# Window attention's values turned by DMA: sixteen transfers in one go, in long pieces, and an earlier wait on TensorE

## The chip, the cores and the metric

The kernel runs on one core of a Trainium2 chip, in 32-bit floating point. The metric is the device time of one execution in microseconds (us); lower is better.

## What is computed

The input x has 16 images of 56 x 56 positions with 384 channels. Two layers follow each other, each added to its input:

```python
x = x + window_attention(group_norm(x))   # 12 heads of 32, windows of 7 x 7, shifted by 3
x = x + depthwise_conv3x3(group_norm(x))  # 3 x 3 weights of +1, 0 or -1 for each channel
```

The attention, for each window of 49 positions and each head:

```python
q, k, v = split(x @ w_qkv.T)                  # 384 -> 3 x 384
score = q @ k.T / sqrt(32) + relative_bias    # 49 x 49, with masks in edge windows
out = softmax(score) @ v                      # 49 x 32
out = out @ w_out.T + b_out
```

The change is about v on its way to the product with the softmax.

## The kernel before, in words

**Tiling.** An image is cut into 8 strips of 7 rows (392 positions, 8 windows). There are 128 strips, numbered s. Each strip has two units of four windows; u = 2s is the first half, u = 2s + 1 the second. A unit takes about 15 us, an image about 242.

**One strip's attention.** TensorE forms queries and keys (`query_key`, L471, tile `pq`) and values (`value`, L483, tile `pv`) with channels on the partitions; ScalarE copies them to `qk` and `vt`. For each unit, `scores` (L515) multiplies keys with queries into `score_banks`, VectorE adds the bias (L546), ScalarE takes the exponential (L564, tile `e`), `add_up` (L592) sums it over the keys with a product by ones (L599), `attend` (L608) multiplies the exponentials with the values (L619, tile `po`), ScalarE copies the result (L629). In between, ScalarE and VectorE invert the sums (L637 to L640), and VectorE multiplies the result with them (L647). After both halves `project` (L649, tile `py`) applies w_out, and VectorE adds the input (L666).

**The values by key.** The product in `attend` needs the values with the keys on the partitions. `turn` (L496) has VectorE transpose 32 x 32 blocks of `vt` into `vq`, where a partition still belongs to a group of 32 channels' heads. `by_key` (L503) then moves blocks of 32 partitions by DMA from `vq` to the tile `v` (two buffers): 16 transfers a strip, each of 32 partitions and 48 KB, in two parts of eight. In `v`, the 32 channels of a head are put at their place among 384, so a transfer's piece is 32 numbers, 128 bytes.

**The order of the work** is written out by hand. `heavy` (L939) lists for each unit six steps; `all_units` (L973) runs a step's list, and between the steps what is planned for that time from the other layers (convolution, loads, stores). In the first unit of strip s, the values of strip s + 1 are formed in steps 0, 1 and 2, turned in steps 1, 2 and 3, and `by_key` comes in step 3 (part 0) and step 5 (part 1). Right after step 0 of each unit come `add_up` and `attend`. So TensorE's order in a first half is: three products of `pv`, the sums, the products with the values, the rest of `pv`, the scores of the next unit, `pq`; in a second half `pq`, sums, products, `pq`, then `py` and scores.

**Queues.** The transfers of `by_key` are issued by SyncE. In the same queue, in the order of the program, lie the convolution's loads of a band (`band`, L705) and its stores (`store`, L800), eight for a chunk. The loads of the next image's strips and the stores of the middle result lie on GpSimd's queue (L421, L682). SyncE takes its instructions one after the other: one that waits holds up those behind it.

**Waits.** The scheduler puts the waits for other engines and for DMAs on the instruction that first needs them. The sixteen transfers of a strip count on eight semaphores, two transfers each. An instruction that has more than one wait gets instructions of its own in front of it, shown as EVENT_SEMAPHORE, which TensorE's sequencer executes. In the kernel before, the values' waits lie on the first eight products of `attend` in a strip's first half.

**The convolution** of image b - 1 goes on beside the attention of image b, mostly on VectorE (`tap`, L786), in chunks of 2.6 units.

Of the kernel before, what the change touches and what calls it, by code (L numbers as in the profile page):

```python
# [9 lines left out]
F32 = mybir.dt.float32  # L10
# [24 lines left out]
def kernel(  # L35
# [12 lines left out]
    nc = tc.nc  # L48
    P = 128
    B, H, W, C = x.shape  # L50
    NH = rel_table.shape[1]
    D = C // NH
    NC = C // P
    HPC = P // D
    T = WIN * WIN
    NS = H // WIN
    NW = W // WIN
    ST = WIN * W
    UW = 4
    UPS = NW // UW  # L60
# [22 lines left out]
    vpool = ctx.enter_context(tc.tile_pool(name="v", bufs=2))  # L83
# [9 lines left out]
    def bank(name):  # L93
        return ps.tile([P, 512], F32, tag="mm", name=name)
# [21 lines left out]
    vq = const.tile([P, 4, NW // 2, NC, D], F32, tag="vq", name="vq")  # L116
# [121 lines left out]
    stats, coefs, parts = {}, {}, {}  # L238
# [124 lines left out]
    xs = {}  # L363
# [93 lines left out]
    vs, ots, pts, ys = {}, {}, {}, {}  # L457
    raw, sums = {}, {}
# [37 lines left out]
    def turn(s, m):  # L496

        nc.vector.transpose(  # L498
            vq[:, :, :, m].rearrange("p h n d -> p n h d"),
            vt[:, m].rearrange("p (n w) (j b) -> p n (w j) b", w=2, b=D),  # L500
        )

    def by_key(s, part):  # L503

        if part == 0:
            vs[s] = vpool.tile([P, NW // 2, C], F32, tag="v", name=f"v_{s}")
        v = vs[s]
        for half in range(2 * part, 2 * part + 2):
            for i in range(HPC):
                nc.sync.dma_start(  # L510
                    v[half * D : (half + 1) * D].rearrange("k n (m c) -> k (n m) c", m=NC)[:, :, i * D : (i + 1) * D],
                    vq[i * D : (i + 1) * D, half].rearrange("k n m d -> k (n m) d"),
                )

    def scores(u, fast):  # L515


        s, n = divmod(u, UPS)
        pp = score_banks
        rows = T if fast else HT  # L520
        for j in range(NC):
            for r in range(2):
                for k in range(2 * HPC):
                    i, w = k % HPC, (k + k // HPC) % 2
                    part = slice(i * D, (i + 1) * D)
                    q0 = (n * UW + 2 * r + w) * T
                    row, col = (w, r) if fast else (r, w)
                    k0 = (2 * j + col) * T
                    nc.tensor.matmul(  # L529
                        pp[row * HT : row * HT + rows, i, k0 : k0 + T],  # L530
                        qk[part, NC * fast + j, q0 : q0 + rows],
                        qk[part, NC * (not fast) + j, q0 : q0 + T],
                        start=True,
                        stop=True,
                    )
        raw[u] = pp
# [50 lines left out]
    def by_head(u):  # L587

        flat = es.rearrange("k h w q -> k (h w q)")[:, : NH * 2 * T]
        return flat.rearrange("k (h r q) -> k h r q", h=NH, r=2)  # L590

    def add_up(u):  # L592

        flat = es.rearrange("k h w q -> k (h w q)")[:, : NH * 2 * T]
        su = raw[u][:, 0:2, : NC * 2 * T]
        for i in range(HPC):
            for w in range(2):
                keys = slice(w * HT, w * HT + T)
                nc.tensor.matmul(  # L599
                    su[i * D : (i + 1) * D, w],  # L600
                    ones[keys, :D],
                    flat[keys, i * NC * 2 * T : (i + 1) * NC * 2 * T],
                    start=True,
                    stop=True,
                )
        sums[u] = su

    def attend(u, fast):  # L608
        s, n = divmod(u, UPS)
        if n == 0:  # L610
            ots[s] = two.tile([P, NC, ST], F32, tag="ot", name=f"ot_{s}")
        po = [bank(f"po_{u}_{w}") for w in range(2)]
        for j in range(NC):
            for r in range(2):
                for i in range(HPC):
                    for w in range(2):
                        h = HPC * j + i
                        keys = slice(w * HT, w * HT + T)
                        nc.tensor.matmul(  # L619
                            po[w][i * D : (i + 1) * D, (2 * j + r) * T : (2 * j + r + 1) * T],  # L620
                            vs[s][keys, n * 2 + r, h * D : (h + 1) * D],
                            by_head(u)[keys, i * NC + j, r] if fast else pts[u, j][keys, 2 * i + r, :],
                            start=True,
                            stop=True,
                        )
        ot = ots[s][:, :, n * UW * T : (n + 1) * UW * T]
        by_window = ot.rearrange("p j (r w q) -> p j r w q", r=2, w=2)
        for w in range(2):
            nc.scalar.copy(  # L629
                by_window[:, :, :, w, :], po[w][:, : NC * 2 * T].rearrange("p (j r q) -> p j r q", j=NC, r=2)  # L630
            )
# [55 lines left out]
    mids, bands, outs, centers = {}, {}, {}, {}  # L687
# [45 lines left out]
    count, padded = [0], {}  # L733
# [205 lines left out]
    def heavy(u):  # L939

        s, half = divmod(u, UPS)
        todo = [[] for _ in range(2 * NC)]
        more = s + 1 < B * NS
        for m in range(NC):
            if half == 0 and more:
                todo[m].append((value, (s + 1, m)))
                todo[m + 1].append((turn, (s + 1, m)))
                todo[NC + m].append((query_key, (s + 1, m)))
            if half and more:
                todo[m].append((query_key, (s + 1, NC + m)))  # L950
            if half:
                todo[NC + m].append((project, (s, m)))
        if more and not half:
            for part in range(2):
                todo[NC + 2 * part].append((by_key, (s + 1, part)))
        if half and s + 2 < B * NS:
            todo[NC + 1].append((normalize, (s + 2,)))
        return todo
# [14 lines left out]
    def all_units(fast):  # L973
        for m in range(2 * NC):
            query_key(0, m)
        scores(0, fast)
        softmax(0, fast)
        for m in range(NC):
            value(0, m)
        normalize(1)  # L980
        exponential(0, fast)
        for m in range(NC):
            turn(0, m)
        for part in range(2):
            by_key(0, part)
        plan(nc.sync)
        for u in range(B * NU):
            todo = heavy(u)
            light = [(w, f, a) for w, f, a in sorted(side.pop(u, []), key=lambda i: i[0])]
            more = u + 1 < B * NU  # L990

            then = NC if u % UPS else NC - 1
            for i in range(len(todo)):
                run(todo[i])
                if i == 0:
                    if fast:
                        add_up(u)
                    else:
                        for j in range(NC):
                            transpose(u, j)  # L1000
                    if fast:
                        invert(u)
                    attend(u, fast)
                    if fast:
                        divide(u)
                if i == then and more:
                    scores(u + 1, fast)
                    softmax(u + 1, fast)
                if i == then + 1 and more:
                    exponential(u + 1, fast)  # L1010
                while light and light[0][0] - u <= (i + 1) / len(todo):
                    _, g, a = light.pop(0)
                    g(*a)
            for _, g, a in light:
                g(*a)
        for _, g, a in sorted((i for u in side for i in side[u]), key=lambda i: i[0]):
            g(*a)
        side.clear()
# [47 lines left out]
    with tc.If(redo != 0):  # L1066
        with tc.manual_schedule():
            staged.clear()
            for kept in (xs, stats, coefs, parts, vs, ots, pts, ys, raw, sums, mids, bands, outs, centers, padded):
                kept.clear()  # L1070
            clear_again()
            load_bias(nc.gpsimd, 0, T, False)
            add_bias(False)
            for s in range(2):
                fetch(s)
            for s in range(NS):
                for c in range(NC):
                    load(s, c)
                if s + 2 < NS:
                    fetch(s + 2)  # L1080
            norm_gather((0, 0), nc.sync)
            norm_scale((0, 0), nc.sync, nc.vector)
            normalize(0)
            all_units(False)
# [44 lines left out]
```

## Time and profile before

| | |
|---|---|
| time, median of 3 runs | 4079.17 us (4078.88 to 4080.06) |
| profiled execution | 4081.16 us, span 4079.4 us |
| TensorE clock granted | 0.991 of full speed, mean |
| busy: PE, PEld, DVE, ACT, POOL | 98%, 60%, 86%, 55%, 46% |
| DMA packets | 1523990, of these 1458970 under 512 bytes |
| transfers v<-vq | 2048 of 48.0 KB |
| waiting instructions of L619 | 949 |

PE is TensorE's matmul, PEld its weight loads, DVE is VectorE, ACT ScalarE, POOL GpSimd, SP SyncE; a q behind the name means the engine's sequencer. A matmul in 32 bits shows as two records of PE and two of PEld: the 48 products of a unit are 96 records. The starts of records are measured; their ends on TensorE are modelled. A row of the timeline gives start, length, engine, line, operation, tiles and the number of records merged, and in brackets the idle time before it with what ended it. The timeline's length of a row runs to the end of its last record.

### The profile page before, as it was taken

What the parts mean: (1) busy time and instruction counts of PE and PEld (TensorE: products, weight loads), DVE (VectorE), ACT (ScalarE), POOL (GpSimd) and SP (SyncE); (2) the same over time, 40 slices, a digit from 0 to 9 for tenths busy, and PEclk for the clock granted to TensorE, in tenths of its full rate; (3) what the DMA queues carried; (4) which work ended last, traced back from release to release, by engine and by line L of the source; (5) the groups of instructions that cost most, each with busy time, mean ns of one, the idle gap of its engine ahead of it and who ended that gap; (6) DMA issues with size and microseconds to landing.
All of it is one profiled execution on the core that took longest, in us unless ns stands there. A gap on an engine that the chain in (4) does not pass through costs nothing.

```text
span 4079.4 us, 144987 instructions
## 1 busy us (share of the span) xinstructions
PE 3981.1 (98%) x63161; PEld 2447.1 (60%) x63161; DVE 3495.8 (86%) x3712; ACT 2231.7 (55%) x4654; POOL 1870.2 (46%) x3165
## 2 busy tenths in 40 slices
PE   5999999999999999999999999999999999999997
PEld 3666666656656666566666666666566566666656
DVE  4555989889898998989889898998989889898897
ACT  2555646555565655656555565655656556565552
POOL 5444535545453554545445452554545455452100
PEclk8999999999999999999999999999999999999998
DMA  4434556655665665556665665655556565664544
GB/s 95 78 62 90 112 102 127 107 109 107 114 114 111 117 111 108 111 99 128 108 116 104 113 117 105 117 117 101 115 101 123 105 124 104 108 123 79 108 102 110
DMA packets 1523990, 438.93 MB, mean 108 GB/s; under 512 B 1458970, under 2 KB 1473979, under 8 KB 1523346
## 3 DMA queue, kind: packets, MB, share of 16 engines
q1 hardware_dynamic: 1432680, 267.66, 38.9%
q0 software_dynamic: 87648, 159.12, 16.4%
q8 instruction: 500, 8.19, 0.9%
q10 hardware_dynamic: 3018, 2.78, 0.3%
q14 instruction: 144, 1.18, 0.1%
HBM read 169.63 MB, written 158.46 MB: 80 GB/s over the span
## 4 chain that ended last, share of the span: by engine, by line
PE 46%; issue 16%; POOL 12%; DVE 12%; DMA 7%; SPq 4%; ACT 2%; DVEq 0%; ACTq 0%; POOLq 0%
PE pq L474 19%; PE pv L487 10%; PE py L658 8%; POOL xl L421 8%; DVE o L786 5%; PE score_banks L529 3%; PE po L619 3%; SPq L510 3%; DMA xl<-in_x_dram 2%; PE score_banks L599 2%; DMA mvd<-mv 2%; DVE e L546 1%; POOL dev L270 1%; DMA gt<-mvd 1%; DVE xt L438 1%
## 5 line engine op out<-in xcount | busy, mean ns | idle before, releaser
L474 PE MATMUL pq<-xn,wq_t 128*128 128x392 f32 x4608 | 1586.7, 497 | 0.1
L421 POOL DMA_DIRECT2D xl<-in_x_dram x1980 | 1329.3, 722 | 153.8 <-DVE xt L438 94.2
L786 DVE SCALAR_TENSOR_TENSOR o<-hp,dw_t,o 128x1568 f32<-128x1568 f32 x752 | 1378.4, 1833 | 5.7 <-DVE o L786 0.5
L474 PEld LDWEIGHTS pq<-xn,wq_t 128*128 128x128 f32 x4608 | 846.1, 188 | 596.1 <-issue 1.4
L487 PE MATMUL pv<-xn,wq_t 128*128 128x392 f32 x2304 | 815.9, 497 | 9.8 <-DVE y L666 8.6
L658 PE MATMUL py<-ot,wo_t 128*128 128x392 f32 x2304 | 818.2, 500 | 4.8 <-DVE ot L647 3.8
L481 ACT COPY qk<-pq 128x392 f32<-128x392 f32 x768 | 368.4, 482 | 609.6 <-PE pq L474 609.3
L678 POOL COPY y<-y 128x63 f32<-128x63 f32 x128 | 59.4, 464 | 1280.5 <-DVE y L666 1280.5
L487 PEld LDWEIGHTS pv<-xn,wq_t 128*128 128x128 f32 x2304 | 424.2, 189 | 309.9 <-DVE y L666 10.4
L658 PEld LDWEIGHTS py<-ot,wo_t 128*128 128x128 f32 x2304 | 425.8, 190 | 306.5 <-DVE ot L647 20.1
L564 ACT ACTIVATE e<-e 128x1176 f32<-128x1176 f32 x256 | 303.3, 1185 | 462.5 <-DVE e L546 461.4
L639 DVE SCALAR_TENSOR_TENSOR ln<-score_banks,inv 128x588 f32<-128x588 f32 x256 | 195.9, 765 | 349.2 <-ACT inv L638 349.2
L494 ACT COPY vt<-pv 128x392 f32<-128x392 f32 x384 | 188.8, 492 | 393.0 <-PE pv L487 392.1
L619 PEld LDWEIGHTS po<-e,v 49*32 49x32 f32 x24576 | 352.2, 105 | 60.4 <-issue 14.3
L619 PE MATMUL po<-e,v 49*32 49x49 f32 x24576 | 347.1, 212 | 13.4 <-DMA v<-vq 11.9
L546 DVE SCALAR_TENSOR_TENSOR e<-score_banks,bias 128x1176 f32<-128x1176 f32 x256 | 347.2, 1356 | 10.7 <-PE score_banks L529 10.7
L529 PEld LDWEIGHTS score_banks<-qk 32*49 32x49 f32 x24576 | 265.7, 118 | 145.4 <-issue 108.9
L450 ACT COPY x<-xt 128x196 f32<-128x196 f32 x720 | 225.5, 368 | 176.0 <-DVE xt L438 175.6
L529 PE MATMUL score_banks<-qk 32*49 32x49 f32 x24576 | 298.2, 218 | 2.6 <-DVE ln L639 2.2
L498 DVE STREAM_TRANSPOSE vq<-vt 128x512 f32<-128x512 f32 x384 | 265.6, 693 | 9.9 <-ACT vt L494 6.4
L463 ACT ACTIVATE xn<-x,coef 128x392 f32<-128x392 f32 x384 | 247.1, 711 | 13.3 <-DMA coef<-cod 13.3
L666 DVE TENSOR_TENSOR y<-py,x 128x392 f32<-128x392 f32 x384 | 213.3, 555 | 43.1 <-PE py L658 39.2
(174 smaller groups left out, 3279.3 us busy)
## 6 DMA issues: line engine op xcount, KB each, us to landing
v<-vq SPq DMA_DIRECT2D x2048, 48.0 KB
xb<-mid SPq DMA_DIRECT2D x90, 855.5 KB
out_dram<-o SPq DMA_DIRECT2D x736, 98.0 KB
mid<-y POOLq DMA_DIRECT2D x112, 619.5 KB
xl<-in_x_dram POOLq DMA_DIRECT2D x1260, 52.5 KB
mid<-y POOLq DMA_DIRECT2D x15, 354.0 KB
xl<-in_x_dram POOLq DMA_DIRECT2D x180, 28.0 KB
mid<-y POOLq DMA_DIRECT2D x15, 265.5 KB
```

The costliest lines, as they stand in the source:

```text
L421: nc.gpsimd.dma_start(xz[i * D + lo : i * D + hi, c, k : k + n, :], flat[token : token + n * (hi - lo)].rearrange("(k t) c -> t k c", k=n) ...
L463: nc.scalar.activation(xn[:, c, :, :T], xs[s][:, c, :].rearrange("p (w t) -> p w t", t=T), AF.Identity, bias=coef[:, c, 1:2], scale=coef[: ...
L474: nc.tensor.matmul(pq[:, :ST].rearrange("p (w t) -> p w t", t=T), wq_t[:, c, m * P : (m + 1) * P], xn[:, c, :, :T], start=(c == 0), stop=( ...
L481: nc.scalar.copy(qk[:, m, :ST], pq[:, :ST])
L487: nc.tensor.matmul(pv[:, :ST].rearrange("p (w t) -> p w t", t=T), wq_t[:, c, 2 * C + m * P : 2 * C + (m + 1) * P], xn[:, c, :, :T], start= ...
L498: nc.vector.transpose(vq[:, :, :, m].rearrange("p h n d -> p n h d"), vt[:, m].rearrange("p (n w) (j b) -> p n (w j) b", w=2, b=D),)
L529: nc.tensor.matmul(pp[row * HT : row * HT + rows, i, k0 : k0 + T], qk[part, NC * fast + j, q0 : q0 + rows], qk[part, NC * (not fast) + j, ...
L546: nc.vector.scalar_tensor_tensor(e, pp[:, :, : NC * 2 * T].rearrange("q i (n k) -> q i n k", k=T), QSCALE, bias[:, int(s % NS == NS - 1)]. ...
L564: nc.scalar.activation(flat, flat, AF.Exp, accum_out=reach[:, 0, u : u + 1])
L619: nc.tensor.matmul(po[w][i * D : (i + 1) * D, (2 * j + r) * T : (2 * j + r + 1) * T], vs[s][keys, n * 2 + r, h * D : (h + 1) * D], by_head ...
L658: nc.tensor.matmul(py[:, :ST], wo_t[:, c, m * P : (m + 1) * P], ots[s][:, c, :], start=(c == 0), stop=(c == NC - 1),)
L786: nc.vector.scalar_tensor_tensor(acc, by_half(hp[:, dy : dy + BR, dx : dx + W]), dw_t[:, c, t : t + 1], acc, ALU.mult, ALU.add)
```

## The change

All sixteen transfers of a strip are issued in one call of `by_key`, in step 3 of the unit. The tile `v` is laid out anew, as key, group of 32 partitions, window pair, third of the heads, channel of the head, so that each partition's 384 numbers of a transfer lie together: the piece is 1536 bytes. `attend` reads the same 32 numbers for each head at their new place. And the first product of `add_up` in a strip's first half is made to wait for all sixteen transfers (but for the very first strip), by a dependency that is added by hand; the products of `attend` behind it then need no wait of their own for them.

```diff
-    def by_key(s, part):
-
-        if part == 0:
-            vs[s] = vpool.tile([P, NW // 2, C], F32, tag="v", name=f"v_{s}")
-        v = vs[s]
-        for half in range(2 * part, 2 * part + 2):
+    carried = {}
+
+    def by_key(s):
+
+        vs[s] = vpool.tile([P, HPC, NW // 2, NC, D], F32, tag="v", name=f"v_{s}")
+        carried[s] = []
+        for half in range(4):
             for i in range(HPC):
-                nc.sync.dma_start(
-                    v[half * D : (half + 1) * D].rearrange("k n (m c) -> k (n m) c", m=NC)[:, :, i * D : (i + 1) * D],
-                    vq[i * D : (i + 1) * D, half].rearrange("k n m d -> k (n m) d"),
+                move = nc.sync.dma_start(
+                    vs[s][half * D : (half + 1) * D, i].rearrange("k n m d -> k (n m d)"),
+                    vq[i * D : (i + 1) * D, half].rearrange("k n m d -> k (n m d)"),
                 )
+                carried[s].append(move.ins.name)
+
+    def await_values(s, product):
+
+        for name in carried.pop(s) if s else ():
+            tc.add_manual_dep(
+                product.ins,
+                name,
+                mybir.DependencyInfo(mybir.DependencyClass.Sync, mybir.DependencyReason.DATA),
+                reason="values by key",
+            )
...
-                nc.tensor.matmul(
+                product = nc.tensor.matmul(
                     su[i * D : (i + 1) * D, w],
                     ones[keys, :D],
...
+                if u % UPS == 0 and i == 0 and w == 0:
+                    await_values(u // UPS, product)
...
-                            vs[s][keys, n * 2 + r, h * D : (h + 1) * D],
+                            vs[s][keys, i, n * 2 + r, j],
...
-            for part in range(2):
-                todo[NC + 2 * part].append((by_key, (s + 1, part)))
+            todo[NC].append((by_key, (s + 1,)))
...
-        for part in range(2):
-            by_key(0, part)
+        by_key(0)
```

More of the change, by code (lines that the diff above doesn't have):

```diff
@@ L616, in attend @@
                     for w in range(2):
-                        h = HPC * j + i
                         keys = slice(w * HT, w * HT + T)
@@ L1068 @@
             staged.clear()
-            for kept in (xs, stats, coefs, parts, vs, ots, pts, ys, raw, sums, mids, bands, outs, centers, padded):
+            for kept in (xs, stats, coefs, parts, vs, ots, pts, ys, raw, sums, carried, mids, bands, outs, centers, padded):
                 kept.clear()
```

## The prediction

> **What bounds the kernel now.** I read the page's busy lines first, then the waits, then single strips in the timeline, since the change touches something that happens once a strip, 128 times.
>
> ```profile
> PE 3981.1 (98%) x63161; PEld 2447.1 (60%) x63161; DVE 3495.8 (86%) x3712; ACT 2231.7 (55%) x4654; POOL 1870.2 (46%) x3165
> ...
> q1 hardware_dynamic: 1432680, 267.66, 38.9%
> ...
> L619 PE MATMUL po<-e,v 49*32 49x49 f32 x24576 | 347.1, 212 | 13.4 <-DMA v<-vq 11.9
> ```
>
> TensorE is busy 98% of the span, so a saving counts only if TensorE itself gets shorter: by less idle time, or by a stretch that it now runs more slowly than it could. The products with the values (L619) show both. Idle before them is only 13.4 us. The slow stretch shows in single units. Here are the sums and products of two first halves of a strip, in the timeline of TensorE (start us, length us):
>
> ```profile
> 1923.33 0.73 PE L599 MATMUL score_banks<-e,ones 49*32 49x294 f32 x16
> 1923.85 1.45 PE L619 MATMUL po<-e,v 49*32 49x49 f32 x96
> ```
>
> ```profile
> 2259.08 0.72 PE L599 MATMUL score_banks<-e,ones 49*32 49x294 f32 x16
> 2259.59 1.14 PE L619 MATMUL po<-e,v 49*32 49x49 f32 x96
> ```
>
> The same 96 records take 1.45 us in one and 1.14 us in the other. What differs is the waiting instructions of line L619 in those windows, 8 against 5:
>
> ```profile
> L619 PEldq EVENT_SEMAPHORE  x8: 51/51/51, 1923.3 to 1924.2; - x8
> ```
>
> ```profile
> L619 PEldq EVENT_SEMAPHORE  x5: 51/51/51, 2259.1 to 2259.6; - x5
> ```
>
> Eight starts over 0.9 us are one every 0.125 us. The first comes at 1923.3, beside the sums; so about 0.5 us of them lie under the sums, which is five, and each further one delays the products by some 0.1 us: with 8 it is 0.31 us. Over the run the line has 949. Counting them strip by strip in the trace gives 98 strips with eight, one with seven, 13 with six and 16 with five (98x8+7+13x6+16x5 = 949). The second half of a strip has none.
>
> Some strips also wait for the data. SyncE's timeline, then TensorE's, for the worst of them:
>
> ```profile
> 1207.06 6.69 SPq L510 DMA_DIRECT2D v<-vq  x8
> 1213.79 2.79 SPq L800 DMA_DIRECT2D out_dram<-o  x4
> 1216.63 6.34 SPq L510 DMA_DIRECT2D v<-vq  x8
> ```
>
> ```profile
> 1222.74 0.25 PE L619 MATMUL po<-e,v 49*32 49x49 f32 x2
> 1223.23 0.72 PE L619 MATMUL po<-e,v 49*32 49x49 f32 x8 [0.24 <-issue]
> 1224.29 1.41 PE L619 MATMUL po<-e,v 49*32 49x49 f32 x86 [0.34 <-DMA v<-vq]
> ```
>
> The second eight transfers start behind four stores, the last is issued at 1222.3, and the products that need it run until 1225.7: 2.95 us instead of 1.14.
>
> **What the Trainium skill says.** "Perfetto Trace Analysis", Identifying Dependency Chains: an instruction that waits on several engines may get EventSemaphore instructions in front of it; the trace agrees, with the 949. The same page, Sequencer-only Instruction: the profile shows only the execution of such an instruction; so I price one by the spacing, 0.125 us, not by its 51 ns. "TensorE: Matmul & The Clock Gate", Architectural detail: TensorE's queue is 64 deep. The trace shows at least 24 records of lead (below). "DMA: Bandwidth & Descriptors", Specifications: pieces under 512 bytes miss the line rate; the queue that moves mostly 128-byte pieces took 0.389 x 4079.4 x 16 / 1432680 = 17.7 ns a packet of 187 bytes on average, so the trace doesn't speak against it.
>
> **The change, part by part.**
>
> *1. Waits leave the products.* In the built program of the changed kernel the first product of a strip's sums carries nine waits (eight DMA semaphores, each covering two transfers, and ScalarE's exponential), and the products carry one each. The five to eight waiting instructions among the products are gone. Against 1.14 us: 97 strips (without the first) x 0.31 = 30.1 us; 13 strips with six, at 0.09 (median 1.032 against 0.941 us from first to last start), 1.2 us; one with seven, 0.2 us. Sum 31.5. But second halves, with no waiting instruction, average 0.10 us over the fastest 0.941, in short gaps that the trace doesn't explain; I expect half of that, 0.05 x 127 = 6.4 us, to come up here. Net 25; ends 18 and 31.5.
>
> *2. Waits appear before the sums.* Nine waits are four waiting instructions (they hold two each in the trace) and one on the product: 4 x 0.125 = 0.5 us a strip if nothing hides them. What hides them is work already queued. The values' products come just ahead of the sums, and this is their waiting instruction of one strip, and TensorE's timeline there:
>
> ```profile
> L487 PEldq EVENT_SEMAPHORE  x1: 51/51/51, 1947.4 to 1947.4; - x1
> ```
>
> ```profile
> 1947.48 4.22 PE L658 MATMUL py<-ot,wo_t 128*128 128x392 f32 x12
> 1951.54 2.14 PE L487 MATMUL pv<-xn,wq_t 128*128 128x392 f32 x6
> ```
>
> It ran at 1947.4, before the first of 12 py products that precede its own, which started 4.1 us later. So TensorE's sequencer is 12 products (24 records with their weight loads) ahead, and reaches the head of the sums some 4 us before they start. Cost: 0, ends 0 and 63 us (127 x 0.5). Queued behind these waits are the sums and products; for them wait ScalarE's Ln (L637), the copies of po (L629), and VectorE's L639.
>
> *3. The stalls on data.* Over strips 1 to 127 the time of the products beyond what eight waiting instructions cost comes to 10.6 us, nearly all in 13 strips whose last issue was within 2 us of the sums. Now the second eight follow the first: at the spacing of 0.62 us, 16 take 9.9 us. In these strips the first is issued 15.2 us before the sums, so the last is 5.3 us before, and landing took 2.1 us in the first strip (last issue 93.1, last products from 95.22). Even 0.5 us earlier, at the sums, it is there. Gain 9, ends 6 and 10.6.
>
> *4. The first strip.* Its products wait for the transfers (5.4 + 2.0 + 0.5 us). The issues run from 82.55 to 93.1, 0.70 us apart; at the 0.62 us of one issue that is 1.2 us less. Gain 1.2, ends 0 and 3.
>
> *5. Pieces of 1536 bytes.* 2048 x 384 = 786432 pieces become 65536. At 17.7 ns they held 16 engines for 870 us at most. The nearest row for long pieces is q10 (3018 packets, 2.78 MB, 0.3%: 65 ns for 921 bytes); by bytes some 108 ns, an estimate, so 65536 x 108 / 16 = 440 us. DMA falls from a half to about 0.4 busy, but nothing on TensorE's path waits for DMA in the steady part except point 3: 0, ends 0 and a gain of 5 (loads of later strips).
>
> *6. Moved past.* On SyncE eight issues (5 us) now go ahead of stores L800, and of a band load L705 where it lay between. The stores free an accumulator used again two chunks, over 70 us, later; the band is planned 0.87 of a 39 us step ahead of its use. 0, ends 0 and a loss of 3.
>
> *7. Who is late next.* VectorE. In the strip at 668 it is nearly full:
>
> ```profile
> 668.00:698.00 30.00, 30.00 (x476) 18.19 (x470) 29.20 (x31) 14.82 (x35) 15.31 (x23) 1.00 0.69 139
> ```
>
> (PE, PEld, DVE, ACT, POOL busy; here 29.2 of 30.0.) Three strips an image are like this, with 0.4 to 1.5 us left in each, against 0.31 us to save, or over 1 us in the strip with the data stall. TensorE already waits 13 times for VectorE's y (L666) before pv, in the third unit of an image; 0.31 us of each such strip turns into wait: 4 us. In the stalled strips I take off 0.3 x 13 = 4. Loss 8, ends 4 and 20.
>
> **Sum.** 25 + 9 + 1.2 - 8 = 27 us. The profiled execution took 4081.2 us (span 4079.4 and 1.8 around it), 2.0 over the median of the runs, 4079.2. So 4054 for that execution, and 4052 on the median; with the small gains of point 5 I put **4051**.
>
> **The rivals.**
>
> *Waits before the sums exposed (slower), 0.06.* If the sequencer reaches them less than 0.1 us ahead, all four instructions show: +63 us, less points 1, 3 and 4, (25 + 9 + 1) = +28: 4107. It decides once more than 0.28 us a strip shows. Against it stand the 4.1 us above; for it, that this lead is seen for a wait of one semaphore only.
>
> *VectorE takes over (small gain), 0.16.* If the full strips and their neighbours give all of it back, half the strips keep their gain: about 13 us, 4066. For: DVE 29.2 of 30; against: from 576 to 818 us, one image, it is busy 217.5 us of 242, so 24 are idle.
>
> *Full gain, 0.25.* No gaps in the first halves, no give-back beyond the pv wait: 31.5 + 10.6 + 1.2 - 4 = 39: 4040.
>
> *Nothing moves, 0.05.* The stretch of 1.45 us could have another cause than the waiting instructions, with the stalls made up elsewhere: 4079. Against it, five against eight within the same kind of unit.
>
> My forecast, 0.48. That the transfers are not merged is out: the built program has them as 32 rows of 384.
>
> **Numbers.** The range reaches from the full gain with a bit of point 5 to the VectorE case: 4033 to 4066. About 0.2% (8 us) is what a measurement here can tell from no change: faster 0.89, same 0.05, slower 0.06.
>
> **What would show it.** Right: no waiting instruction at L632 (the products' new line) in steady strips, four at the sums' line L611 some microseconds before the sums, products 1.14 to 1.27 us, no idle time before them from v<-vq after the first strip, q1 with about 712,000 packets, the wait of pv for y longer than 8.6 us. Wrong: idle time before the sums, or po short and the units as long as before with waits for DVE.

## The result, and the profile after

The changed kernel takes 4051.1 us (median of 4 runs, 4050.0 to 4052.3) against 4079.2 us before: a ratio of 0.993 (95% interval 0.9918 to 0.9942), or 28 us less. Run again beside later kernels, it was 0.9923 (0.9910 to 0.9937). Its profiled execution took 4050.03 us, with a span of 4048.2 us, 31.1 us under the span before.

From the page after: the engines' busy time, SyncE's DMA queue, and the products (now line L632).

```profile
PE 3948.1 (98%) x63161; PEld 2408.9 (60%) x63161; DVE 3495.5 (86%) x3712; ACT 2227.4 (55%) x4654; POOL 1858.7 (46%) x3165
...
q1 hardware_dynamic: 711784, 267.66, 30.4%
...
L632 PE MATMUL po<-e,v 49*32 49x49 f32 x24576 | 311.0, 212 | 7.2 <-DMA v<-vq 7.0
```

TensorE does the same 63161 matmul records in 33 us less, and the products alone are 36 us shorter (347.1 to 311.0). (Busy time rests on modelled ends; the table of starts below is measured.) The waiting instructions among the products, in the view of that line over the run, are those of the very first strip only:

```profile
L632 PEldq EVENT_SEMAPHORE  x8: 51/51/51, 86.2 to 92.9; - x8
```

A first half in TensorE's timeline after, and the waiting instructions of the sums' line (L611) in a window from 1880 to 1910 us around it:

```profile
1907.97 0.73 PE L611 MATMUL score_banks<-e,ones 49*32 49x294 f32 x16
1908.49 1.14 PE L632 MATMUL po<-e,v 49*32 49x49 f32 x96
```

```profile
L611 PEldq EVENT_SEMAPHORE  x4: 51/51/51, 1906.1 to 1906.4; - x4
```

The products take 1.14 us. The four waits run 1.9 to 1.6 us before the sums start, while TensorE still works on the values. The strip of the first kernel that was shown with late data, now in SyncE's timeline:

```profile
1197.43 12.64 SPq L511 DMA_DIRECT2D v<-vq  x16
1210.11 4.43 SPq L813 DMA_DIRECT2D out_dram<-o  x6
```

The stores come behind all sixteen transfers. The sums of this strip start at 1212.58, and nothing waits for data.

What became longer are TensorE's waits for VectorE. From the waits of TensorE after (total us, times, longest):

```profile
PE pv L487 <- DVE y L679: 14.0, 16, 1.2
...
PE py L671 <- DVE ot L660: 7.8, 16, 3.0
```

The same lines before:

```profile
PE pv L487 <- DVE y L666: 8.6, 13, 0.7
...
PE py L658 <- DVE ot L647: 3.8, 5, 3.0
```

Adding up the starts of TensorE's records, strips 1 to 126, after minus before:

| stretch | change, us |
|---|---|
| products of first halves, first to last start (163.1 to 118.5) | -44.6 |
| last value matmul to first sum (52.9 to 53.0) | 0.0 |
| products of first halves to the next pv (26.3 to 31.9) | +5.6 |
| products of second halves (131.1 to 134.6) | +3.4 |
| rest of the second halves (1634.7 to 1641.4) | +6.6 |
| rest of the first halves | -0.5 |
| up to the second strip, and after the last but one | -3.0 and +1.2 |

The sum is -31.3; the span says -31.1.

### The profile page after: what moved, and what is told of

Read it like the earlier page. It is cut to its first block, busy times and chain, and to the rows that moved or that the text cites. A ratio compares the mean times of both kernels' runs of the same rounds, so it can differ in the third digit from the quotient of the medians.

```text
span 4048.2 us, 144624 instructions
## 1 busy us (share of the span) xinstructions
PE 3948.1 (98%) x63161; PEld 2408.9 (60%) x63161; DVE 3495.5 (86%) x3712; ACT 2227.4 (55%) x4654; POOL 1858.7 (46%) x3165
## 3 DMA queue, kind: packets, MB, share of 16 engines
q1 hardware_dynamic: 711784, 267.66, 30.4%
## 4 chain that ended last, share of the span: by engine, by line
PE 33%; issue 22%; POOL 18%; DVE 16%; DMA 8%; ACT 2%; SPq 1%; DVEq 0%; ACTq 0%; POOLq 0%
POOL xl L421 13%; PE pq L474 13%; PE pv L487 7%; PE py L671 7%; DVE o L799 6%; PE score_banks L541 2%; PE po L632 2%; DMA mvd<-mv 2%; DVE xt L438 2%; DVE e L558 2%; DMA xl<-in_x_dram 2%; PE score_banks L611 1%; POOL dev L270 1%; SPq L511 1%; DMA cod<-both 1%
## 5 line engine op out<-in xcount | busy, mean ns | idle before, releaser
L632 PEld LDWEIGHTS po<-e,v 49*32 49x32 f32 x24576 | 311.8, 105 | 58.7 <-issue 8.2
L632 PE MATMUL po<-e,v 49*32 49x49 f32 x24576 | 311.0, 212 | 7.2 <-DMA v<-vq 7.0
L463 ACT ACTIVATE xn<-x,coef 128x392 f32<-128x392 f32 x384 | 247.0, 711 | 13.2 <-DMA coef<-cod 13.2
```

The source lines that it names most:

```text
L463: nc.scalar.activation(xn[:, c, :, :T], xs[s][:, c, :].rearrange("p (w t) -> p w t", t=T), AF.Identity, bias=coef[:, c, 1:2], scale=coef[: ...
L632: nc.tensor.matmul(po[w][i * D : (i + 1) * D, (2 * j + r) * T : (2 * j + r + 1) * T], vs[s][keys, i, n * 2 + r, j], by_head(u)[keys, i * N ...
```

## The experiments

Theory A is that of the prediction: the waiting instructions among the products cost most, and late data some 10 us. Theory B: late data and the traffic of short pieces cost most. Each kernel below was timed beside the kernel before on its chip, and ratios are to that. Totals in us for strips 1 to 126 are added up from the records of one profiled execution, as above (that of w_alone took 4090 us, 6 more than its median): the products of the first halves, and what the sums start later than 0.42 us behind the last value matmul ("idle before sums").

| kernel | us | ratio (95%) | products | idle before sums |
|---|---|---|---|---|
| wait only (w_alone) | 4084.2 | 1.0008 (1.0001 to 1.0015) | 120.0 | 30.9 |
| one go only (g_alone) | 4082.6 | 1.0003 (0.9995 to 1.0011) | 163.6 | 0 |
| long pieces only (p_alone) | 4077.3 | 0.9992 (0.9986 to 0.9999) | 156.6 | 0 |
| wait and pieces (wp) | 4070.9 | 0.9976 (0.9965 to 0.9987) | 121.8 | 17.2 |
| wait and one go (wg) | 4055.1 | 0.9931 (0.9917 to 0.9944) | 118.8 | 0 |
| one go and pieces (gp) | 4083.4 | 0.9999 (0.9991 to 1.0008) | 163.9 | 0 |
| all three (after_again) | 4050.6 | 0.9923 (0.9910 to 0.9937) | 118.6 | 0 |

**The wait alone**, on two parts and short pieces.

```diff
...
+                if u % UPS == 0 and i == 0 and w == 0:
+                    await_values(u // UPS, product)   # the sums' first product, all 16 transfers
...
```

> The kernel before, with the first product of a strip's sums made to wait for all sixteen transfers; still two parts of eight and pieces of 128 bytes. Theory A (waiting instructions among the products cost most of it): products of the first halves at 0.94 us from first to last start in all strips, 34 us less there; but the strips whose second eight come late now wait in front of the sums, 13 x 0.5 us more than before; VectorE gives some 6 us back. About 4058 us (4050 to 4066). Theory B (late data and the DMA traffic cost most of it): no gain, since the data are as late as before: 4079 to 4086.

It gained nothing: 1.0008. The time is theory B's, and theory A's 4058 us is missed by 26. But the products are as short as in the changed kernel (120.0 against 118.5 us), as theory A has it; TensorE now stands still before the sums instead. From its waits over the run, and its timeline and SyncE's in one strip:

```profile
PE score_banks L612 <- DMA v<-vq: 17.2, 11, 2.6
```

```profile
2197.43 2.14 PE L487 MATMUL pv<-xn,wq_t 128*128 128x392 f32 x6
2201.60 0.73 PE L612 MATMUL score_banks<-e,ones 49*32 49x294 f32 x16 [2.03 <-DMA v<-vq]
```

```profile
2184.36 5.81 SPq L512 DMA_DIRECT2D v<-vq  x8
2190.21 2.94 SPq L814 DMA_DIRECT2D out_dram<-o  x4
2193.20 6.20 SPq L512 DMA_DIRECT2D v<-vq  x8
```

Starts tell it: 30.9 us in 21 strips, where the data stalls before were 10.6 us. An earlier wait makes late data dearer. Before, the sums (0.52 us) and the waiting instructions (0.34 us) ran while the data were still under way; 21 x 0.86 = 18 us more, and 10.6 + 18 is about the 31. I had expected 6.5 us more, for 13 strips.

The 31 us alone don't use up the 43 by which the products got shorter. A second cost goes with late sums, in TensorE's granted clock. In the strip shown, the twelve value records behind the products took 5.52 us, where the changed kernel took 4.22 from 1879.59 on; the window from 2202.60 to 2206.00, with its granted clock third from the end, shows TensorE at half clock:

```profile
2203.38 5.52 PE L487 MATMUL pv<-xn,wq_t 128*128 128x392 f32 x12
```

```profile
2202.60:2206.00 3.40, 3.40 (x75) 2.16 (x63) 1.84 (x3) 3.37 (x6) 0.79 (x2) 0.50 0.53 184
```

Between 130 and 3940 us this execution has eight such stretches at half clock, 3.4 us long and once 6.8. Each begins beside sums that were 1.5 to 2.6 us late, from 0.1 us before they start to 1.8 us after, though some sums as late have none. The kernel before has no such stretch there, and the changed one has none in its steady part. In these eight strips the rest of the first halves took 12.1 us longer than the median. So the balance of this execution is 43 us less in the products, 31 more before the sums, 12 more at half clock, 5 more before the next pv and 4 more in the second halves: 9 us more, as its span is (4088.2 against 4079.4). That standing still brought the lower clock is read from where the stretches lie; no run tested it by itself.

**One go alone**, and **one go with long pieces**.

```diff
-            for part in range(2):
-                todo[NC + 2 * part].append((by_key, (s + 1, part)))
+            todo[NC].append((by_key, (s + 1,)))
```

> The kernel before with all sixteen transfers issued in one go; pieces of 128 bytes, waits on the products. Theory A: the data stalls go (10 us), but the built program has sixteen transfer waits among the products in every strip, where the kernel before had fewer in 29 of them: up to 8 us more. About 4077 us (4071 to 4081). Theory B: 4055 to 4065.

> The changed kernel without the added wait: one go, pieces of 1536 bytes, waits on the products again. Theory A: the eight waiting instructions are back in every first half, 0.31 to 0.34 us in 127 strips; only the stalls and the first strip are gained: about 4075 us (4069 to 4081). Theory B (data and traffic): 4051 to 4058.

Neither gained: 1.0003 and 0.9999. Both lie outside theory A's ranges (4082.6 against 4071 to 4081 us, 4083.4 against 4069 to 4081), by the chips' own level (the kernel before took 4081.3 and 4084.2 there), not by their ratios. The data stalls are gone in both, but so are the strips with fewer waits; the line of the products in g_alone, over the run:

```profile
L630 PEldq EVENT_SEMAPHORE  x1024: 51/51/51, 87.3 to 3967.5; - x171
```

1024 is eight in each of 128 strips, where there were 949. Why 30 strips had fewer isn't shown; perhaps the first part's landing was already known to TensorE there through another wait, which one go rules out. So 163.1 us became 163.6: what the stalls gave (10.6), the added waits took (some 9 us, an estimate from the medians: 0.34 us in 16 strips and 0.25 in 13). Theory B is out: with data in time and long pieces, the kernel isn't faster.

**Long pieces alone, and with the wait.**

```diff
-            vs[s] = vpool.tile([P, NW // 2, C], F32, tag="v", name=f"v_{s}")
+            vs[s] = vpool.tile([P, HPC, NW // 2, NC, D], F32, tag="v", name=f"v_{s}")
...
```

> The kernel before with pieces of 1536 bytes; two parts, waits on the products. Theory A: transfers issue and land sooner, so the data stalls shrink by some 3 us and the first strip by 2: about 4075 us (4070 to 4079); the eight waiting instructions stay. Theory B: the DMA traffic matters by itself: 4060 or less.

> The changed kernel with the transfers in two parts again (waits in front of the sums, pieces of 1536 bytes). Theory A: about 4055 us (4049 to 4062): like the changed kernel, but with idle time before the sums in the 13 strips whose second part comes late. Theory B: 4065 to 4075.

p_alone gained 3 us, as theory A has it, but as a balance: its first halves' products are 6.5 us shorter, and its second halves' products 6.5 us longer (137.6 against 131.1). gp has 137.1 where g_alone has 130.8. So something about the long pieces, or the layout of `v` that comes with them, costs the second halves time; what it is stays open. wp is a miss of theory A (4071 against 4049 to 4062), in theory B's range: with two parts, 17.2 us of idle time before the sums are left of the 30.9. So long pieces help where data are late: 4084 to 4071 us from w_alone to wp. A transfer lands only a little sooner after its issue: where the sums were over 0.3 us late, they started 2.63 us after the last issue in w_alone and 2.51 in wp (medians). More comes from the last issue itself, which lies 1.43 us instead of 0.99 ahead of the time at which the sums could have started (means of every eighth strip from 13 to 117, where the data are latest); and two stretches at half clock are left of eight. Late data do count as theory B says, once the wait stands before the sums.

**Wait and one go, short pieces.**

> The changed kernel with pieces of 128 bytes (one go, waits in front of the sums). Theory A: pieces matter only in the first strip and a little in how soon the data land: 4053 us (4050 to 4058). Theory B (DMA traffic): 4062 or more.

4055.1 us, as theory A has it. To the whole change there are 3 us (0.9931 against 0.9923), not clear of the intervals. With one go, pieces hardly matter: the last issue is 2.6 us or more ahead of the sums in every steady strip.

**Half the wait.** The sums wait for the first eight transfers only; four products of a first half wait for the rest.

```diff
-        for name in carried.pop(s) if s else ():
+        for name in carried.pop(s)[:8] if s else ():
```

> The changed kernel, but the sums wait only for the first eight transfers; four products of a first half wait for the other eight. Four or so waiting instructions stay among the products. Theory A (the first five are covered by the sums, further ones cost 0.1 us each): nothing is lost, 4051 us (4048 to 4055), products at 0.94 to 1.0 us. Rival C (every waiting instruction there costs its share, 0.34 / 8 = 0.04 us): 127 x 4 x 0.04 = 21 us more before give-back, 4062 to 4072.

4051.7 us, 0.9922 (0.9908 to 0.9935): no loss, though the views of both lines show as many waiting instructions among the products as before the sums:

```profile
L632 PEldq EVENT_SEMAPHORE  x516: 51/51/51, 85.0 to 3929.2; - x172
```

```profile
L611 PEldq EVENT_SEMAPHORE  x508: 51/51/51, 117.1 to 3924.8; - x170
```

Four a strip are free, and the products take 119.0 us as without them. Rival C, in which each has its price, is out: the first ones run under the sums; before, with eight, it was those beyond the fifth that cost. Its first halves show the steps: with five waiting instructions the products took 0.94 us from first to last start in the median, with six 1.03, in the one strip with seven 1.13, and with eight 1.28.

**What came back.** One tap of the convolution (of eight beside the centre) is left out for all images but the last; so these two compute less than the reference.

```diff
-                at(when + step * i / 9, tap, p, k, c, t)
+                if t:
+                    at(when + step * i / 9, tap, p, k, c, t)
```

> The kernel before with one of the eight off-centre taps of the convolution left out for all images but the last. Theory A: TensorE's 13 waits for VectorE's y go (9 us): about 4069 us, and the same omission in the changed kernel brings more than here. Rival D: both become shorter by the same.

> The changed kernel with one of the eight off-centre taps of the convolution left out for all images but the last (about 1.83 us less of VectorE in each chunk of 2.6 units). To be set against the kernel before with the same left out. Theory A (what came back is TensorE waiting for VectorE's y and ot): the distance between the two grows from 28 to 38 us or more; this one at about 4030 us. Rival D (it came back for another cause): the distance stays at 28.

The kernel before gained 4 us (0.9992, 0.9983 to 1.0000), the changed one 9 (0.9901, 0.9886 to 0.9916, against 0.9923 and 0.9922 for the changed kernel and its half wait). The distance between the two kernels grew from 31 us (0.9923) to some 37. That is 6 us, and the intervals of the two ratios together leave some 7 us open: the direction is A's, but the growth isn't clear of the noise. The totals are also mixed: leaving the tap out took 9.0 us of stalls from the products of the kernel before (163.1 to 154.1), and added 11.3 us to the rest of its first halves and 5.8 to those of the changed kernel, in pauses before the scores whose cause stays open. By the stretch it is clearer. The rest of the second halves fell by 13.2 us in the changed kernel (1641.4 to 1628.2), with py's wait for ot down from 7.8 to 3.0, and by 5.8 in the kernel before, so the 6.6 us between the two are gone. That part of the give-back is VectorE's load. But pv's waits for y stayed, 8.6 and 14.1 us; there theory A was wrong. VectorE's timeline after, where pv waits, shows the cause:

```profile
602.51 0.56 DVE L679 TENSOR_TENSOR y<-py,x 128x392 f32<-128x392 f32 x1
603.10 0.57 DVE L685 BATCH_NORM_STATS2 st<-y 128x6 f32<-128x392 f32 x1
604.70 0.57 DVE L454 BATCH_NORM_STATS2 st<-x 128x6 f32<-128x392 f32 x1 [1.02 <-ACT x L453]
605.18 1.83 DVE L799 SCALAR_TENSOR_TENSOR o<-hp,dw_t,o 128x1568 f32<-128x1568 f32 x1
606.93 0.56 DVE L679 TENSOR_TENSOR y<-py,x 128x392 f32<-128x392 f32 x1
```

```profile
607.55 4.22 PE L487 MATMUL pv<-xn,wq_t 128*128 128x392 f32 x12 [1.19 <-DVE y L679]
```

The last y of the strip stands in VectorE's order behind a statistic that waits 1.02 us for ScalarE, and behind a tap. It isn't the load, it is the order. So the last two kernels put these two behind y.

```diff
-                at(when + 0.2 + 0.2 * c, arrange, s, c)
+                at(when + 0.2 + (0.2 if r else 0.36) * c, arrange, s, c)
...
-                at(when + step * i / 9, tap, p, k, c, t)
+                at(when + step * i / 9 + (0.15 if n == NB * NC - 1 and i == 6 else 0), tap, p, k, c, t)
```

> The changed kernel itself once more, beside the other two on one chip: 0.993 of the kernel before, about 4052 us.

> The changed kernel with two pieces of VectorE's work put behind the last y of a strip, at the place where TensorE's pv waits for it in the third unit of an image: a statistic of the loads' arrangement (0.57 us, and 1.0 us of waiting for ScalarE in front of it) and one tap (1.83 us). Theory A (what came back there is this order on VectorE, not VectorE's load): the 14 us of pv's waits go nearly all, about 4040 us (4036 to 4046). Rival D (VectorE as a whole is too full, the wait only moves): 4050 us, with waits for ot or e in place of y.

> The kernel before with the same reordering of VectorE. Theory A: its 8.6 us of pv's waits go, about 4071 us, so that the distance to the reordered changed kernel is some 5 us larger than between the two without it: 33 us instead of 28. Rival D: 4079.

after_y takes 4038.4 us (4036.7 to 4039.2), 0.9892 (0.9876 to 0.9907) of the kernel before: 12 us less than the changed kernel on the same chip, and the fastest of all. Of pv's 14.0 us of waiting for y, 0.6 are left:

```profile
PE py L671 <- DVE ot L660: 6.6, 12, 3.0
...
PE pv L487 <- DVE y L679: 0.6, 3, 0.2
```

before_y gains 10 us (0.9974, 0.9965 to 0.9983). The distance between the reordered pair is 34 us, against 31 without the reordering on that chip. It was expected to grow by 5 us; 2 to 3 are within the intervals, so this growth isn't shown.

## Why the prediction was right, and where it was not

The time (4051) and the sign came out as forecast. That the median was met to the microsecond is in part luck: the sum was made for a profiled execution, where it gave 4054 and the measured one took 4050, and several steps below missed in opposite directions. By its steps:

1. *Waits leave the products:* 25 us net, at most 31.5. Measured: 44.6 us with the stalls, so 34.0 without them, over the upper end. The term that failed is the 6.4 us taken off for gaps: the first halves show none, 0.94 us in the median. The rest is the price of eight waiting instructions: 1.28 us in the median against 0.94, 0.34 us rather than 0.31.
2. *Waits before the sums:* 0. Measured 0.0 us. Over the strips, the first of the four ran 1.4 to over 6 us before the sums, 5.7 in the median. In one strip such a wait held TensorE's sequencer for 4.4 us and the sums still started on time. One word of that step was wrong: the lead is 12 matmul records with 12 weight loads, which is six products in 32 bits, not twelve. This agrees with what the Trainium skill says of a queue ahead of the array ("TensorE: Matmul & The Clock Gate", Architectural detail), though against its 64 places the trace shows a lead of 35 records at most: 17 matmuls and 18 weight loads that start between the first of the four waits and the sums.
3. *Stalls on data:* 9. Measured 10.6, all of it. The margin was thinner than reckoned: sixteen issues took 11.0 us in the median strip and 12.6 in the one shown, not 9.9, so the last issue came 3.1 us before the sums there, not 5.3.
4. *First strip:* 1.2. The second strip starts 3.0 us earlier, 0.9 of it already before the first strip's sums; so 2.1, inside the ends.
5. *Long pieces:* 0. About 3 us between wg and the whole, not clear of the intervals. SyncE's queue holds the engines for 30.4 instead of 38.9% of the span, 360 us less; 430 were estimated. In that queue a packet of 128 bytes took 14.7 ns in the mean before, and one of 1536 bytes 97 ns after, against the estimates of 17.7 and 108. The price in the second halves (the experiment with long pieces alone) wasn't foreseen.
6. *Moved past on SyncE:* 0, and no new wait behind it shows.
7. *VectorE late next:* 8. Measured 5.6 before pv and 6.6 in the second halves, 12 in all, inside the ends of 4 to 20. The steps' split was off: 5.6 for the 4 before pv, and 6.6 in the second halves, where the prediction had 4 for the strips with late data. Its reading of how full VectorE is was too tight: in the windows over one image the fullest strips leave it 0.8 to 1.9 us of some 30, not 0.4 to 1.5. The cause before pv was VectorE's order and not its load. Also 3.4 us came back in longer gaps among the products of second halves, which the long pieces bring with them.

So two errors met: nine too little in step 1, and nearly eight too little taken off in step 7 and the second halves. What the sum hid is that steps 1 and 3 don't add: each alone is worth nothing (w_alone, g_alone). One go takes away the stalls, but its sixteen waits fill every strip; the early wait takes the waits out, but turns each late transfer into idle time of the whole engine and, it seems, into a lower clock behind it. Each pays for the other's cost. The prediction treated them as independent gains, and came out right because both were made.

## What to carry to other kernels

A wait put earlier on an in-order engine is free while the work queued ahead of it is longer than the wait, and only if the data are there: bring the data forward first, then gather the waits, and look at the granted clock behind every stand-still that is left. Look for waiting instructions inside dense runs of short matmuls, count them against what the stretch before can cover, and price only the excess. When the bound engine gets shorter, look at the next engine's order as well as at its load: moving two instructions behind the one that is waited for gave 12 us more.

## What was not expected of the hardware

TensorE's sequencer takes about 0.125 us for a waiting instruction with a product behind it, and 0.11 us for each of several in a row (four within 0.32 us, from 1906.08 to 1906.40). Five of them in front of 48 products were covered by 0.52 us of sums, with no trace in the time, and eight cost 0.34 us. A transfer of 48 KB was issued in 589 ns with 32 pieces and in 618 ns with 384, and landed about as soon (2.51 and 2.63 us from the last issue to the late sums, in wp and w_alone): cutting a transfer finely cost its issue and its landing little here, though its packets held the DMA engines for longer. And a stand-still of TensorE of 2 us was followed by 3.4 us at half clock in several strips.
